# Half of the scaled copies on another engine, and lasting buffers for the decay, in a fused Mamba and convolution kernel

## The chip, the cores and the metric

The kernel runs on one core of one Trainium2 chip. The core has five engines that run their own instruction queues in order: PE (TensorE, matrix products and transposes), DVE (VectorE), ACT (ScalarE), POOL (GpSimd) and SP (SyncE, which here only issues DMAs). The metric is the device time of one execution in microseconds (us). The kernel before took 19,451.17 us, the median of three runs from 19,447.44 to 19,455.76.

In the profile PE stands for matrix products, PEld for the weight loads before them, and L12 for line 12 of the kernel.

## The reference

The input x is 4 images of 256 x 64 positions with 128 channels, all in float32. Two layers are added to it, each on a group-normalised input.

Layer 0 is a two-directional Mamba block. Each of the 64 columns of an image is a sequence of T = 256 steps. After a layer norm and a projection to 256 inner channels there comes, for each direction, a causal convolution over four taps, a SiLU, projections to a step size, and to vectors B and C of 16 states, and the selective scan:

```python
def step(h, inp):
    u_t, d_t, B_t, C_t = inp
    dA = jnp.exp(d_t[..., None] * A)
    h = dA * h + (d_t * u_t)[..., None] * B_t[:, None, :]
    y = jnp.einsum('bdn,bn->bd', h, C_t)
    return (h, y)
```

The backward direction runs the same on the reversed sequence. The two results are summed, gated and projected back; layer norms and a small MLP follow.

Layer 1 makes queries, keys and values with two products, normalises them, convolves keys and values with 3 x 7 windows into small per-position matrices, and multiplies these per position.

## The kernel before

**Tiling.** Two sequences (SG = 2) of 256 steps make a tile of 512 columns. With 256 inner channels in two halves of 128 partitions, a group G is two sequences; there are 32 groups an image and 128 in all. For each group the scan is run for 2 directions (i) and 16 states (n). One such pass is a **unit**: 128 x 32 = 4096 units, numbered k.

**What a unit does.** `rows_of_c` (L476) fetches a row of C over all partitions with a DMA from SP. `inputs` (L481) makes two operands of the scan. The first is du times B: du lies transposed, with positions on the partitions (tile duT, four blocks of 128 x 256), so that B of a block is one number a partition; ACT multiplies each block by it into the tile dbt (L487, four instructions). The second is the decay exp(A dt): ACT computes it for each half of the channels (L493, two instructions). At the start of each of the two sequences the decay must be 0, so that nothing is carried over from one to the next; since the exponential writes 255 of 256 steps, a memset on POOL (L491) sets the missing one: the first step for the forward direction, the last for the backward one. The tile "decay" comes anew from a pool of four buffers for every unit, so the memset is repeated for every unit.

`turned` (L502) transposes dbt back on PE into a PSUM bank, channels on partitions, in four 128 x 128 pieces a half (L507). Three banks, dbs, take turns. `scanned` (L510) runs the recurrence as one scan instruction a half on DVE (L519), from the decay in SBUF and dbt in PSUM; the backward direction reads and writes reversed views. `weighted` (L521) multiplies both halves by C on POOL in one instruction (L525). `added` (L527) transposes the product into the PSUM tiles y, where it accumulates over states and directions (L547).

**Order.** The main loop (from L1006) writes unit k's steps with a lead: in pass k it calls `inputs` for unit k + 3 (AHEAD = 3) after `weighted(k)`, and `added` for unit k - 2 (LAG = 2) after the transposes of unit k + 1. Between these calls it steps generators that hold all other work: `front` for the next group (norm, convolution, projections, softplus, du on POOL at L433), `back` for a finished group, `project` and `mix` for layer 1 of the images that are done. In the first image there is no layer 1 beside the scans. Where those are written decides only a first order: a scheduler in the tile framework sets the final order of each engine's queue by its own model, and puts in the semaphore waits. In the order built for the kernel before, the memset for unit k + 3 mostly stands just ahead of unit k's product on POOL.

**The end.** When all units are done, `mix_alone` (L882) works off what is left of layer 1 (136 of the 512 blocks of 128 positions). There the pool's tiles dbt and decay are reused for other data: `pair("decay")` (L935) takes two of them, which POOL fills (L938, recorded at L779).

Of the kernel before, what the change touches and what calls it, by code (L numbers as in the profile page):

```python
# [13 lines left out]
F32 = mybir.dt.float32  # L14
AF = mybir.ActivationFunctionType
ALU = mybir.AluOpType
# [16 lines left out]
COLS = 512  # L33
# [6 lines left out]
def fused_kernel(ctx: ExitStack, tc: tile.TileContext, a: dict, out: bass.AP):  # L40
    nc = tc.nc
    x = a["x"]
    B, T, N, _ = x.shape
    SG = COLS // T
# [3 lines left out]
    CB = COLS // 128  # L48
# [5 lines left out]
    AHEAD, LAG = 3, 2  # L54
# [120 lines left out]
    keep = ctx.enter_context(tc.tile_pool(name="keep", bufs=1))  # L175
# [3 lines left out]
    p4 = ctx.enter_context(tc.tile_pool(name="p4", bufs=4))  # L179
# [3 lines left out]
    dbs = [psum.tile([128, COLS], F32, name=f"db{k}") for k in range(3)]  # L183
# [3 lines left out]
    for t in hpad:  # L187
        nc.gpsimd.memset(t[:, :, 0 : KC - 1], 0.0)
        nc.gpsimd.memset(t[:, :, T + KC - 1 : PADT], 0.0)
    kv_pad = keep.tile([32, R, PADN], F32, name="kv_pad")  # L190
    nc.gpsimd.memset(kv_pad, 0.0)
    cols = [[keep.tile([128, 2, COLS], F32, name=f"cols{t}") for t in range(3)]]
# [14 lines left out]
    def take():  # L207
        return free.pop(0)

    def give(*bs):  # L210
        free.extend(bs)
# [269 lines left out]
    def inputs(G, i, n):  # L481

        st = state[G]
        dt, bT, duT = st["dt", i], st["bT"], st["duT", i]
        dbt = st["dbt", i, n] = p4.tile([128, CB, DI], F32, name="dbt")
        for j in range(CB):
            nc.scalar.mul(dbt[:, j, :], duT[:, j, :], bT[:, i, j, n : n + 1])  # L487
        da = st["da", i, n] = p4.tile([128, 2 * SG, T], F32, name="decay")
        lo = 1 - i

        nc.gpsimd.memset(da[:, :, (T - 1) * i : (T - 1) * i + 1], 0.0)  # L491
        for h in range(2):
            nc.scalar.activation(  # L493
                da[:, h * SG : (h + 1) * SG, lo : lo + T - 1],
                dt[:, h, :].rearrange("d (s t) -> d s t", s=SG)[:, :, lo : lo + T - 1],
                AF.Exp,
                scale=neg_a[i][:, h, n : n + 1],
            )
        if n == NS - 1:
            st[("half", "read")[i]] = True  # L500
# [9 lines left out]
    def scanned(k):  # L510
        G, i, n = units[k]
        st = state[G]
        hs = st["hs", i, n] = p4.tile([128, 2, COLS], F32, name="hs")
        da = st.pop(("da", i, n)).rearrange("d (h s) t -> d h (s t)", h=2)
        for h in range(2):
            d0, d1, dh = da[:, h, :], dbs[(2 * k + h) % 3], hs[:, h, :]
            if i == 1:
                d0, d1, dh = d0[:, ::-1], d1[:, ::-1], dh[:, ::-1]
            nc.vector.tensor_tensor_scan(dh, d0, d1, 0.0, ALU.mult, ALU.add)  # L519
# [209 lines left out]
    def operands(K):  # L729

        b, ci = divmod(K, NCHK)
        w = chunk[K]
        img = kv_img[b % 2]
        to = w["cols"] = cols[0]
        cols.append(cols.pop(0))
        for i in range(2):
            for t in range(3):
                c0, cn = CH0[t], CH0[t + 1] - CH0[t]
                src = img[16 * i + c0 : 16 * i + c0 + cn, :, ci * R * N : ci * R * N + COLS + 2 * N]
                tap = src.ap[1][0]  # L740
                src = bass.AP(src.tensor, src.offset, [[tap, KW * cn], [N, KH], [1, COLS]])
                nc.sync.dma_start(out=to[t][0 : TAPS * cn, i, :], in_=src)
        w["operands"] = True

    def ready(K):
        w = chunk.get(K, {})
        return w.get("projected") and (K % NCHK == NCHK - 1 or chunk.get(K + 1, {}).get("projected"))
# [28 lines left out]
    def outer(eng, pr, left, right, na, nb):  # L776

        n = pr.shape[1]
        eng.tensor_tensor(  # L779
            pr.rearrange("p e (a b) -> p e a b", b=nb),  # L780
            left[:, :, :, None].to_broadcast([128, n, na, nb]),
            right[:, :, None, :].to_broadcast([128, n, na, nb]),
            ALU.mult,
        )
# [15 lines left out]
    def by(ap, inner=16):  # L800
        return ap.rearrange("p (e a) -> p e a", a=inner)

    def loaded_x1(K):
        x1 = p1.tile([128, CB, C], F32, name="x1t")
        nc.sync.dma_start(out=x1, in_=chunk_of(im[K // NCHK]["x1d"], K % NCHK))
        return x1
# [75 lines left out]
    def mix_alone(first, project):  # L882

        blocks = [(K, j) for K in range(first, B * NCHK) for j in range(CB)]
        wk = [{} for _ in blocks]

        def pair(name):
            return [p4.tile([128, 8, 128], F32, name=name) for _ in range(2)]

        def needed(K):  # L890
            while not ready(K):
                project()
            if "operands" not in chunk[K]:
                operands(K)

        x1 = o = None
        for m in range(-1, len(blocks) + 3):
            project()
            w1 = wk[m - 1] if 0 <= m - 1 < len(blocks) else None
            w2 = wk[m - 2] if 0 <= m - 2 < len(blocks) else None  # L900
            w3 = wk[m - 3] if 0 <= m - 3 < len(blocks) else None
            if w3:
                K, j = blocks[m - 3]
                if x1 is None:
                    x1 = loaded_x1(K)
                if j == 0:
                    o = p1.tile([128, CB, C], F32, name="o")
                pr = pair("dbt")
                for h in range(2):
                    outer(nc.vector, pr[h], by(w3["vg"][:, 256:512])[:, 8 * h : 8 * h + 8], by(w3["nv"], NH)[:, 8 * h : 8 * h + 8], DV, NH)  # L910
                give(w3["vg"])
            project()
            if w1:
                bank = take()
                gathered(bank[:, 0:128], *w1["pr"])
                kt = p1.tile([128, NH * DD], F32, name="ker")
                nc.scalar.copy(kt, bank[:, 0:128])
            if w2:
                pr2 = products(w2["vg"][:, 0:256], w2["ker"], DV, NH)
                w2["nv"] = p1.tile([128, DV * NH], F32, name="nv")  # L920
                nc.vector.tensor_reduce(w2["nv"].rearrange("p (v n) -> p v n", n=NH), pr2, AX.X, ALU.add)
            project()
            if m + 1 < len(blocks):
                K, j = blocks[m + 1]
                w = wk[m + 1]
                if j == 0:
                    needed(K)
                if j == 2 and ready(K + 1) and "operands" not in chunk[K + 1]:
                    operands(K + 1)
                kb = take()  # L930
                convolved(kb[:, 0:256], 0, K, j, True)
                ks = p2.tile([128, CB, DI], F32, name="duT")[:, 0, :]
                nc.scalar.copy(ks, kb[:, 0:256])  # L933
                give(kb)
                w["pr"] = pair("decay")  # L935
                q = chunk[K]["qkv"][:, j, 0 : NH * DK].rearrange("p (n k) -> p k n", k=DK)
                for h in range(2):
                    outer(nc.gpsimd, w["pr"][h], q[:, 8 * h : 8 * h + 8], by(ks)[:, 8 * h : 8 * h + 8], NH, DD)  # L938
                if j == CB - 1:
                    chunk[K]["mixed"] = True  # L940
            project()
            if w1:
                nc.tensor.transpose(bank[:, 128:256], kt, ident)
                w1["ker"] = p1.tile([128, NH * DD], F32, name="ker2")
                nc.scalar.copy(w1["ker"], bank[:, 128:256])
                give(bank)
            if w3:
                K, j = blocks[m - 3]
                ot = take()
                gathered(ot[:, 0:128], *pr, x1[:, j : j + 1, :])  # L950
                nc.scalar.copy(o[:, j, :], ot[:, 0:128])
                give(ot)
                if j == CB - 1:
                    x1 = None
            project()
            if w1:
                K, j = blocks[m - 1]
                w1["vg"] = take()
                convolved(w1["vg"][:, 0:256], 1, K, j, True)
                convolved(w1["vg"][:, 256:512], 2, K, j, False)  # L960
            project()
            if w3 and blocks[m - 3][1] == CB - 1:
                for _ in finish(blocks[m - 3][0], o):
                    pass
# [36 lines left out]
    for k in range(AHEAD):  # L1001
        rows_of_c(*units[k])
        inputs(*units[k])
    for h in range(2):
        turned(0, h)
    for k in range(len(units) + LAG):  # L1006
# [10 lines left out]
        if k < len(units):  # L1017
            scanned(k)
            weighted(k)
# [8 lines left out]
        if k + AHEAD < len(units):  # L1028
            inputs(*units[k + AHEAD])
# [97 lines left out]
```

## Time and profile before

| | us |
|---|---|
| median of three runs | 19,451.17 |
| span of the profiled execution | 19,460.2 |
| PE busy in it | 16,890.9 (87%) |
| ACT busy | 16,112.6 (83%) |
| DVE busy | 15,851.8 (81%) |
| POOL busy | 11,465.8 (59%) |

The profiled execution's own time is its span, from the first to the last instruction; it lies within 0.05% of the median. The mean granted TensorE clock was 0.960 of full speed. A busy PE is not a PE at its peak, since matmuls are pipelined and their ends are modelled. A group's line in the profile gives, in this order, the code line, the engine and operation, the tiles written and read with their shapes, the count, the busy time in us and the mean ns of one, and last the idle time of that engine just before these instructions with what ended it. A line of the waits gives who waited, for which instruction, the us in total, how many times, and the longest.

### The profile page before, as it was taken

The page shows a single profiled execution, that of the slowest core. Times are in us where ns is not written, and L with a number is a line of the kernel's source. Part 1 is how long each engine was busy: PE and PEld are TensorE (multiplying, and loading weights), DVE is VectorE, ACT ScalarE, POOL GpSimd, SP SyncE. Part 2 cuts the span into 40 slices and gives each one's busy share as a digit, 9 for nine tenths or more (in the row PEclk, how much of TensorE's full clock was granted, in tenths as well). Part 3 has the DMA queues.
Part 4 walks back from the last instruction along what each step waited for, and adds up shares of the span by engine and source line. Part 5 has one row for each costly group of instructions (what it writes and reads, how often), then busy time and mean ns, then how long its engine had stood idle before and what let it go on. Part 6 is the DMA issues. An engine that isn't in the chain of part 4 may idle for free. (4 is left out here: it accounts for less than half of the span.)

```text
span 19460.2 us, 309441 instructions
## 1 busy us (share of the span) xinstructions
PE 16890.9 (87%) x109614; PEld 13040.6 (67%) x109614; DVE 15851.8 (81%) x13054; ACT 16112.6 (83%) x31415; POOL 11465.8 (59%) x9129
## 2 busy tenths in 40 slices
PE   6999888888888888888888888888888888888788
PEld 4666666666666666666666666666666666666677
DVE  5777777768888888888888888887888888888778
ACT  6999999998888888888888888888888888888432
POOL 4777677765556555555655555555555555565444
PEclk9999999999999999999999999999999999999899
DMA  2232223223322322322332223222232232332222
GB/s 76 86 87 86 80 81 81 80 80 87 82 80 85 85 81 80 87 81 81 87 90 84 75 80 84 77 79 78 82 83 78 78 87 78 80 87 77 73 71 65
DMA packets 1321088, 1574.83 MB, mean 81 GB/s; under 512 B 343232, under 2 KB 704880, under 8 KB 1319536
## 3 DMA queue, kind: packets, MB, share of 16 engines
q1 hardware_dynamic: 1318000, 1554.40, 28.6%
q8 instruction: 865, 14.17, 0.3%
q14 instruction: 687, 5.63, 0.1%
q10 hardware_dynamic: 1536, 0.63, 0.0%
HBM read 1420.15 MB, written 134.45 MB: 80 GB/s over the span
## 5 line engine op out<-in xcount | busy, mean ns | idle before, releaser
L525 POOL TENSOR_TENSOR hs<-hs,cc 128x1024 f32<-128x1024 f32 x4096 | 9703.4, 2372 | 6728.4 <-issue 2796.6
L519 DVE TENSOR_TENSOR_SCAN hs<-decay,db 128x512 f32<-128x512 f32 x8192 | 9513.7, 1204 | 1651.0 <-PE db L507 1125.9
L487 ACT ACTIVATE dbt<-duT,bT 128x256 f32<-128x256 f32 x16384 | 7066.9, 500 | 359.7 <-PE db L507 354.7
L493 ACT ACTIVATE decay<-dt,neg_a 128x510 f32<-128x510 f32 x8192 | 5451.5, 713 | 560.5 <-DVE hs L519 536.0
L507 PE MATMUL db<-ident,dbt 128*128 128x128 f32 x32768 | 4956.8, 282 | 958.7 <-DVE hs L519 861.8
L507 PEld LDWEIGHTS db<-ident,dbt 128*128 128x128 f32 x32768 | 3847.6, 145 | 2461.2 <-DVE hs L519 1291.2
L547 PE MATMUL y<-ident,hs 128*128 128x128 f32 x32768 | 4460.9, 279 | 25.0 <-POOL hs L525 22.8
L547 PEld LDWEIGHTS y<-ident,hs 128*128 128x128 f32 x32768 | 3853.1, 144 | 210.2 <-issue 150.4
L374 PE MATMUL mm<-hpad,w_cv 128*128 128x512 f32 x4096 | 1921.8, 597 | 70.2 <-ACT u L313 36.5
L768 DVE TENSOR_TENSOR pr<-qkv,mm 128x2048 f32<-128x2048 f32 x372 | 849.8, 2284 | 631.3 <-PE mm L763 393.4
L374 PEld LDWEIGHTS mm<-hpad,w_cv 128*128 128x128 f32 x4096 | 711.6, 190 | 678.6 <-issue 578.1
L779 DVE TENSOR_TENSOR pr<-mm,nv 128x2048 f32<-128x2048 f32 x374 | 850.7, 2275 | 131.8 <-PE mm L763 90.1
L768 DVE TENSOR_TENSOR pr<-mm,ker 128x2048 f32<-128x2048 f32 x413 | 937.7, 2270 | 15.3 <-PE mm L763 13.2
L864 DVE TENSOR_REDUCE nv<-pr 128x128 f32<-128x2048 f32 x376 | 851.9, 2266 | 1.1
L853 DVE TENSOR_REDUCE ker<-pr 128x128 f32<-128x2048 f32 x376 | 851.2, 2264 | 0.4
L790 PE MATMUL mm<-ident,pr 128*128 128x128 f32 x5968 | 754.6, 278 | 105.6 <-DVE pr L779 90.7
L790 PEld LDWEIGHTS mm<-ident,pr 128*128 128x128 f32 x5968 | 676.4, 143 | 229.2 <-DVE pr L779 103.2
L779 POOL TENSOR_TENSOR decay<-qkv,duT 128x1024 f32<-128x1024 f32 x272 | 544.9, 2030 | 406.2 <-ACT duT L933 273.2
L433 POOL TENSOR_TENSOR du<-dt,u 128x1024 f32<-128x1024 f32 x256 | 607.0, 2371 | 297.6 <-ACT dt L322 191.7
L446 PE MATMUL mm<-ident,du 128*128 128x128 f32 x2048 | 377.0, 303 | 290.4 <-POOL decay L491 149.5
L218 ACT ACT_TABLE_LOAD x419 | 537.6, 1283 | 6.8
L534 PEld LDWEIGHTS y<-diag_d,u 128*128 128x128 f32 x4096 | 495.6, 200 | 60.2 <-ACT yt L564 32.7
(288 smaller groups left out, 18950.8 us busy)
## 6 DMA issues: line engine op xcount, KB each, us to landing
cc<-cd SPq DMA_DIRECT2D x4096, 256.0 KB
cols<-kv_img SPq DMA_DIRECT2D x444, 210.0 KB
xin<-in_x SPq DMA_DIRECT2D x256, 256.0 KB
kv_img<-kv_pad SPq DMA_DIRECT2D x896, 64.0 KB
cols<-kv_img SPq DMA_DIRECT2D x222, 252.0 KB
xst<-in_x SPq DMA_DIRECT2D x128, 256.0 KB
x1d<-ot SPq DMA_DIRECT2D x256, 128.0 KB
xt<-x1d SPq DMA_DIRECT2D x128, 256.0 KB
```

What stands on the lines that cost most here:

```text
L374: nc.tensor.matmul(cv.rearrange("c (s t) -> c s t", s=SG), lhsT=w_cv[i][:, k, h * 128 : (h + 1) * 128], rhs=hp[:, :, o : o + T], start=k == 0,
L487: nc.scalar.mul(dbt[:, j, :], duT[:, j, :], bT[:, i, j, n : n + 1])
L493: nc.scalar.activation(da[:, h * SG : (h + 1) * SG, lo : lo + T - 1], dt[:, h, :].rearrange("d (s t) -> d s t", s=SG)[:, :, lo : lo + T - ...
L507: last = nc.tensor.transpose(db[:, 128 * j : 128 * (j + 1)], dbt[:, j, 128 * h : 128 * (h + 1)], ident)
L519: nc.vector.tensor_tensor_scan(dh, d0, d1, 0.0, ALU.mult, ALU.add)
L525: nc.gpsimd.tensor_tensor(hs, hs, cc[:, None, :].to_broadcast([128, 2, COLS]), ALU.mult)
L547: nc.tensor.matmul(y[j // 2][:, j % 2, h, :], lhsT=hs[:, h, 128 * j : 128 * (j + 1)], rhs=ident, is_transpose=True, start=False, stop=i == ...
L768: nc.vector.tensor_tensor(pr, left.rearrange("p (a e) -> p a e", e=16)[:, :, None, :].to_broadcast([128, na, nb, 16]), right.rearrange("p ...
L779: eng.tensor_tensor(pr.rearrange("p e (a b) -> p e a b", b=nb), left[:, :, :, None].to_broadcast([128, n, na, nb]), right[:, :, None, :].t ...
L790: nc.tensor.matmul(to, lhsT=p, rhs=ident, is_transpose=True, start=k == 0, stop=stop and k == len(blocks) - 1, skip_group_check=True,)
L853: nc.vector.tensor_reduce(ker.rearrange("p (n d) -> p n d", d=DD), pr, AX.X, ALU.add)
L864: nc.vector.tensor_reduce(nv.rearrange("p (v n) -> p v n", n=NH), pr, AX.X, ALU.add)
```

## The change

`inputs` gives two of the four copies of a unit (blocks j = 2 and 3) to POOL, as a `tensor_scalar` with the same per-partition number. The decay no longer comes from the pool: four tiles of 1028 columns are made once and set to 0 as a whole on POOL, at the start, and handed round in turn. The exponential always writes steps 1 to 255 of each sequence of 256 columns. Forward units read the tile from column 0, backward units from column 1, so a written 0 stands at the start of each sequence in the sense of the scan either way, and the memset of every unit is gone. `mix_alone` takes its "decay" pairs from the same four tiles.

```diff
+    decays = [keep.tile([128, 2 * SG * T + 4], F32, name=f"decays{k}") for k in range(AHEAD + 1)]
+    for t in decays:
+        nc.gpsimd.memset(t, 0.0)
...
         for j in range(CB):
-            nc.scalar.mul(dbt[:, j, :], duT[:, j, :], bT[:, i, j, n : n + 1])
-        da = st["da", i, n] = p4.tile([128, 2 * SG, T], F32, name="decay")
+            b_n = bT[:, i, j, n : n + 1]
+            if j < CB // 2:
+                nc.scalar.mul(dbt[:, j, :], duT[:, j, :], b_n)
+            else:
+                nc.gpsimd.tensor_scalar(dbt[:, j, :], duT[:, j, :], b_n, None, ALU.mult)
+        da = decays[0]
+        decays.append(decays.pop(0))
         lo = 1 - i
-
-        nc.gpsimd.memset(da[:, :, (T - 1) * i : (T - 1) * i + 1], 0.0)
+        st["da", i, n] = da[:, i : i + 2 * COLS]
         for h in range(2):
             nc.scalar.activation(
-                da[:, h * SG : (h + 1) * SG, lo : lo + T - 1],
+                da[:, h * COLS : (h + 1) * COLS].rearrange("d (s t) -> d s t", s=SG)[:, :, 1:T],
                 dt[:, h, :].rearrange("d (s t) -> d s t", s=SG)[:, :, lo : lo + T - 1],
                 AF.Exp,
                 scale=neg_a[i][:, h, n : n + 1],
...
-        da = st.pop(("da", i, n)).rearrange("d (h s) t -> d h (s t)", h=2)
+        da = st.pop(("da", i, n))
         for h in range(2):
-            d0, d1, dh = da[:, h, :], dbs[(2 * k + h) % 3], hs[:, h, :]
+            d0, d1, dh = da[:, h * COLS : (h + 1) * COLS], dbs[(2 * k + h) % 3], hs[:, h, :]
...
         def pair(name):
+            if name == "decay":
+                ts = [decays.pop(0) for _ in range(2)]
+                decays.extend(ts)
+                return [t[:, 0:1024].rearrange("d (e a) -> d e a", e=8) for t in ts]
             return [p4.tile([128, 8, 128], F32, name=name) for _ in range(2)]
```

## The prediction

> **What bounds the kernel now.** I read the busy time by stages first, because the whole-span shares (PE 87%, ACT 83%, DVE 81%, POOL 59%) average over stages with different limits. In the table each engine has its busy us in a stretch and, in brackets, its instructions.
>
> ```profile
> core 0: us, PE busy (x) PEld busy (x) DVE busy (x) ACT busy (x) POOL busy (x), PEclk, DMA share, GB/s
> 500.00:4800.00 4300.00, 3856.52 (x24455) 2874.37 (x24453) 3300.36 (x3240) 4118.43 (x7992) 2978.60 (x2413) 0.97 0.29 83
> 4800.00:9300.00 4500.00, 3934.73 (x25448) 3018.44 (x25448) 3816.00 (x3019) 3842.99 (x7460) 2601.69 (x2104) 0.96 0.30 83
> 9300.00:13800.00 4500.00, 3880.89 (x25063) 2992.93 (x25063) 3760.11 (x2970) 3780.81 (x7327) 2544.67 (x2062) 0.96 0.29 81
> 13800.00:18110.00 4310.00, 3755.47 (x24275) 2890.15 (x24273) 3648.68 (x2861) 3662.98 (x7116) 2485.00 (x2010) 0.96 0.29 81
> 18240.00:19460.00 1220.00, 1042.20 (x8047) 963.06 (x8045) 972.86 (x606) 368.25 (x886) 618.43 (x333) 0.92 0.25 71
> ```
>
> There are three regimes. Up to 4800 us (stage 1: the first image, no second layer beside it) ACT is 96% busy and is the bound. From 4800 to 18,110 us (stage 2) PE, ACT and DVE are all at 84 to 87%: nobody is full, and time goes in handing work over. After 18,110 us (the end piece) the changed lines don't run. One pass of the inner loop, a "unit" (one direction and one of 16 states for one pair of sequences), has one L525 product on POOL: that line counts 1148 of them in 500 to 4800 us, and 976, 957 and 931 in the three windows of stage 2. So a unit takes 4300/1148 = 3.746 us in stage 1 and 13,310/2864 = 4.647 us in stage 2.
>
> The groups give a unit's work: four dbt copies and two exponentials on ACT, two scans on DVE, one product and one memset on POOL.
>
> ```profile
> L525 POOL TENSOR_TENSOR hs<-hs,cc 128x1024 f32<-128x1024 f32 x4096 | 9703.4, 2372 | 6728.4 <-issue 2796.6 <-ACT dbt L487 862.1 <-DVE hs L519 738.1
> L487 ACT ACTIVATE dbt<-duT,bT 128x256 f32<-128x256 f32 x16384 | 7066.9, 500 | 359.7 <-PE db L507 354.7 <-DVE duT L315 1.1
> L493 ACT ACTIVATE decay<-dt,neg_a 128x510 f32<-128x510 f32 x8192 | 5451.5, 713 | 560.5 <-DVE hs L519 536.0 <-DVE bT L414 14.7 <-POOL qkv L712 7.3
> L491 POOL MEMSET decay<- 128x4 f32 x4096 | 435.8, 108 | 118.1 <-DVE hs L519 101.5 <-ACT dbt L487 16.5
> ```
>
> A dbt copy has a mean of 500 ns but neighbours overlap: 7066.9/16384 = 0.431 us of ACT each. That ACT is what PE waits for in stage 1 is seen in order of time: ACT goes from L487 to L493 to L487 without a gap, 3.02 us a unit where nothing else comes between, and the weight loads of the transposes wait for it.
>
> ```profile
> 2513.30 1.71 ACT L487 ACTIVATE dbt<-duT,bT 128x256 f32<-128x256 f32 x4
> 2513.99 0.14 PEld L507 LDWEIGHTS db<-ident,dbt 128*128 128x128 f32 x1 [0.24 <-ACT dbt L487]
> 2514.91 1.32 ACT L493 ACTIVATE decay<-dt,neg_a 128x510 f32<-128x510 f32 x2
> 2516.14 1.70 ACT L487 ACTIVATE dbt<-duT,bT 128x256 f32<-128x256 f32 x4
> 2516.68 0.14 PEld L507 LDWEIGHTS db<-ident,dbt 128*128 128x128 f32 x1 [0.28 <-ACT dbt L487]
> ```
>
> The waits of stage 2 (here 4800 to 9300 us) read otherwise: PE waits mostly for a scan to free one of three PSUM banks, DVE waits for PE, and ACT itself waits.
>
> ```profile
> DVE hs L519 <- PE db L507: 271.4, 154, 8.4
> PE db L507 <- DVE hs L519: 243.8, 251, 3.6
> ACT decay L493 <- DVE hs L519: 170.9, 162, 3.3
> ```
>
> **The change, part by part.**
>
> *ACT loses two dbt copies a unit.* 2 x 0.431 = 0.86 us. ACT work a unit goes from 4118.43/1148 = 3.59 to 2.73 us in stage 1, and from 11,286.8/2864 = 3.94 to 3.08 us in stage 2.
>
> *POOL gains two copies a unit, at a price X that the trace does not show.* No POOL instruction here multiplies one tensor by a per-partition number. From below: a memset of 256 elements, which reads nothing.
>
> ```profile
> L106 POOL MEMSET w<- 128x256 f32 x1 | 0.3, 306 | 0.0
> masks.py:199 POOL TENSOR_SCALAR_AFFINE_SELECT ident<-ident 128x128 f32<-128x128 f32 x1 | 0.3, 296 | 0.0
> L79 POOL TENSOR_SCALAR_AFFINE_SELECT group_c<-group_c 128x128 f32<-128x128 f32 x1 | 0.5, 520 | 0.0
> L589 POOL TENSOR_TENSOR xo<-xo,xg 128x512 f32<-128x512 f32 x128 | 163.7, 1279 | 40.6 <-DVE xo L586 40.6
> ```
>
> From above: the two-input product. L589 (512 elements, 1279 ns) and L525 (1024, 2372 ns) lie on 0.19 us + 2.13 ns an element, so 0.73 us for 256. Nearest is the flat one-input select of the identity, 296 ns for 128: with the same 0.19 us of start, 0.83 ns an element, so 0.40 us for 256; L79's select with a two-level pattern would give 0.85 us, but dbt and duT slices are flat. I add 0.05 us for fetching the per-partition number (an estimate, no row shows it) and take X = 0.45 us, ends 0.31 and 0.73.
>
> Here a rule speaks against the change. The Trainium skill's page "GPSIMD Engine Reference" says (section 4.1, Engine selection) not to do elementwise arithmetic there, about 2x slower than VectorE, yet that one-input operations run at about line rate; section 3.1 has 2.6 cycles an element for two inputs and 1.8 for a tight loop, at 1.2 GHz. The trace agrees on two inputs (2.13 ns is 2.56 cycles). For one input the page gives, with the trace's 0.19 us start, about 0.41 us (near one cycle) or 0.57 us (1.8 cycles), estimates. The select row sides with the first. POOL's work a unit in stage 1 is 2978.6/1148 = 2.595, less the memset's 0.107, plus 2X: 3.31, 3.39 or 3.63 us for X = 0.41, 0.45 or 0.57, against 3.746 now. By row and by line rate the change gains in stage 1; by 1.8 cycles it gains nothing there.
>
> *The memset goes.* 4096 x 0.107 us of POOL, in the sum above, and with it a wait: each scan and each exponential needed a POOL memset standing behind L525 products. Little hung on it (DVE's wait for L491 is 25.9 us in all). Four memsets of 128x1028 at the start, 4 x 0.95 us by L194's 128x1024, lie before 200 us, where POOL has 10 us of work: nothing; 4 us if uncovered. Four decay buffers rotate as before, and ACT may now write one half when the scan of that half is done. No DMA is added.
>
> *Waits that come in.* In the built order the POOL copies for unit k+4 stand mostly just ahead of the product of unit k (65% of them; 19% are for k+3, 11% for k+5). They wait until PE has transposed unit k, which that product needs anyhow, so queue order alone costs little. Behind POOL's copies stand L525 (then PE's L547) and du (L433, then PE's L446). PE's L507 needs both halves of dbt, some three to four units after POOL writes them, so POOL may lag about a unit before PE stands. PE's waits for POOL are now 124 us in stage 1 and 30 + 100 + 62 = 192 us in stage 2.
>
> **The sum.** *Stage 1:* the fullest engine after is POOL with 3.39 us a unit, PE next with 3856.5/1148 = 3.36, DVE 2.87, ACT 2.73. ACT alone at the top reached 96%; two engines as close as these I put at 94.5%: 3.39/0.945 = 3.585, gain 0.16 x 1148 = 185 us. *Stage 2:* after, PE 4.04, DVE 3.92, POOL 2.665 - 0.107 + 0.90 = 3.46 (74%), ACT 3.08 of 4.647 us. PE and DVE stay the bound; what can go is lateness of ACT: DVE's waits ended by ACT lines (75 + 95 + 113 = 283 us) and PE's (77 + 58 + 48 = 183), 466 us. ACT's slack, which works off the backlog after a run of table loads and SiLU, grows from 15% to 34%, so I take 60%: 280 us. Against it PE's 192 us of waits for POOL, growing by the load 74/57, 60 us. Net 220. *End piece and first 500 us:* nothing, or under 20 us. Sum 405 us off a span of 19,460.2; that execution lies 9 us above the median of 19,451.2, so on the median 19,046, say **19,045 us** (-2.1%).
>
> **The rivals.**
>
> *POOL becomes the bound (slower).* If X is near 0.73, stage 1 has 2.488 + 1.46 = 3.95 us on POOL; at 96% that is 4.11 us a unit, +0.37 x 1148 = +420 us; in stage 2 POOL reaches 2.558 + 1.46 = 4.02, level with PE and DVE, three engines in line again with POOL's products late for PE, say +0.05 x 2864 = +140. About 20,000 us. For: the page's "slower" rule, L79's 520 ns. Against: the flat select's 296 ns. It decides from X of about 0.6, where stage 1 gives (2.488 + 1.2)/0.945 = 3.90, +180 us, and eats what stage 2 gains.
>
> *The hand-over goes too (much faster).* If the waits between PE and DVE in stage 2 are the echo of ACT's bursts (the three scans that a late dbt holds up), PE sets the pace there at 95%: 4.04/0.95 = 4.25, -0.39 x 2864 = -1120 us, with stage 1's 230: 18,100; half of it 18,700. For: PE's weight loads wait 621 us for ACT in stage 2. Against: ACT stands idle 15% there, waiting for PE and DVE.
>
> *Nothing to see.* Stage 1 passes from ACT to POOL at the same pace (X near 0.53 does it) and stage 2 is held by three banks alone: 19,450 us.
>
> **How the numbers follow.** Forecast 54%, much faster 14%, nothing 6%, slower 26%. Faster by over 0.2% (about what a measurement of this kernel can tell from no change): 0.68; within: 0.06; slower: 0.26. The forecast's own range is 18,700 to 19,400 (X from 0.40 to 0.52, stage 2 from nothing to twice the gain). The range reaches down to 18,500, past half of the second rival, and up to 19,780, X near 0.67, leaving out about one in ten at each end.
>
> **What would show it.** POOL's new line at 0.40 to 0.52 us, 8192 of them; ACT near 75% in stage 1 and 66% in stage 2; a unit of about 3.6 us in stage 1 and 4.57 in stage 2; PE's waits for ACT's dbt mostly gone, those for POOL up. Wrong if the POOL line is over 0.6 us, if PE's L547 waits long for L525, or if stage 2 moves by several per cent though PE and DVE keep their work.

## The result, and the profile after

The changed kernel takes 20,754.3 us (median of four runs, 20,735.7 to 20,777.2) against 19,449.3 us: 1.0669 times the kernel before, 95% interval 1.0654 to 1.0684. The forecast was 19,045 us with a range up to 19,780. The profiled execution has a span of 20,734.0 us, 1274 us more than before. Almost none of that lies at the end: from the start of the last product on POOL to the end of the span it is 1348 us before (18,111.8 to 19,460.2) and 1350 us after (19,384.3 to 20,734.0).

The windows that were shown of the kernel before, with each engine's busy us and its instructions in brackets:

```profile
core 0: us, PE busy (x) PEld busy (x) DVE busy (x) ACT busy (x) POOL busy (x), PEclk, DMA share, GB/s
500.00:4800.00 4300.00, 3447.41 (x20700) 2574.96 (x20699) 2815.09 (x2807) 2834.49 (x4818) 4294.74 (x3080) 0.93 0.23 70
4800.00:9300.00 4500.00, 3809.05 (x24071) 2943.34 (x24069) 3557.25 (x2841) 3031.38 (x5268) 4108.15 (x2943) 0.94 0.26 78
9300.00:13800.00 4500.00, 3816.00 (x24502) 2929.43 (x24502) 3672.20 (x2909) 3068.45 (x5306) 4124.62 (x2956) 0.96 0.27 80
```

POOL is busy for 4294.7 of 4300 us in the first window, and 91 to 92% of the time in the other two, where it was at 57 to 58%. ACT fell to 66% and 67 to 68%.

These windows are fixed in time, but the stages are not. Layer 1 begins beside the scans at product 1103 to 1105 in every run: at 4238 us before, at 4973 us after. So the first window, which the prediction takes for the first image alone, holds some 125 units with layer 1 before and none after, and what it says of a unit is not quite like for like. The losses are therefore also counted by units, from the trace's product starts: product 1216 (counted from 0), which lies a little behind the start of layer 1 in all runs, starts at 4723.6 us before and at 5487.0 us after. Of the 1274 us, 763 are lost up to product 1216, 509 from there to the last product, and the rest at the end.

The groups name the reason:

```profile
L532 POOL TENSOR_TENSOR hs<-hs,cc 128x1024 f32<-128x1024 f32 x4096 | 9684.5, 2369 | 726.3 <-issue 210.1
L494 POOL TENSOR_SCALAR dbt<-duT,bT 128x256 f32<-128x256 f32 x8192 | 7493.6, 931 | 472.3 <-PE db L514 420.0
L492 ACT ACTIVATE dbt<-duT,bT 128x256 f32<-128x256 f32 x8192 | 3741.3, 499 | 1401.7 <-PE db L514 1203.6
L554 PE MATMUL y<-ident,hs 128*128 128x128 f32 x32768 | 4643.4, 286 | 1261.0 <-POOL hs L532 1258.2
```

A copy on POOL takes 0.931 us, twice the 0.45 us of the prediction and beyond its upper end of 0.73. The product beside it has kept its price (2369 ns, before 2372). POOL's queue in stage 1, in order of time, has no gap; a product and two copies make 4.13 us, where ACT's turn was 3.02 us before (a unit's copies and exponentials, shown in the prediction):

```profile
2517.08 2.35 POOL L532 TENSOR_TENSOR hs<-hs,cc 128x1024 f32<-128x1024 f32 x1
2519.41 1.82 POOL L494 TENSOR_SCALAR dbt<-duT,bT 128x256 f32<-128x256 f32 x2
2521.21 2.35 POOL L532 TENSOR_TENSOR hs<-hs,cc 128x1024 f32<-128x1024 f32 x1
2523.54 1.82 POOL L494 TENSOR_SCALAR dbt<-duT,bT 128x256 f32<-128x256 f32 x2
2525.34 2.35 POOL L532 TENSOR_TENSOR hs<-hs,cc 128x1024 f32<-128x1024 f32 x1
```

In the same stretch PE stands still until the products come, and so its next transposes (L514) come late:

```profile
2523.61 1.09 PE L554 MATMUL y<-ident,hs 128*128 128x128 f32 x8 [1.41 <-POOL hs L532]
2524.54 1.04 PE L514 MATMUL db<-ident,dbt 128*128 128x128 f32 x8
2527.74 1.86 PE L554 MATMUL y<-ident,hs 128*128 128x128 f32 x8 [2.16 <-POOL hs L532]
```

The scans then wait for PE. The waits from 500 to 4800 us (who waited for whom, us in total, times, longest), after:

```profile
DVE hs L526 <- PE db L514: 804.2, 540, 7.5
PE y L554 <- POOL hs L532: 479.5, 334, 4.5
ACT dbt L492 <- PE db L514: 478.4, 346, 4.9
```

The first of them was, in that window of before:

```profile
DVE hs L519 <- PE db L507: 323.1, 284, 7.8
```

By windows a unit takes 4300/996 = 4.317 us in stage 1 (before 3.746) and, over 4800 to 13,800 us, 9000/1869 = 4.815 us in stage 2 (before 9000/1933 = 4.656).

### The profile page after: what moved, and what is told of

The parts are those of the page before. It is cut to its first block, busy times and chain, and to the rows that moved or that the text cites. A ratio compares the mean times of both kernels' runs of the same rounds, so it can differ in the third digit from the quotient of the medians.

```text
span 20734.0 us, 303196 instructions
## 1 busy us (share of the span) xinstructions
PE 17191.4 (83%) x109614; PEld 13321.3 (64%) x109614; DVE 15886.4 (77%) x13054; ACT 13313.0 (64%) x23233; POOL 18591.4 (90%) x13229
## 5 line engine op out<-in xcount | busy, mean ns | idle before, releaser
L526 DVE TENSOR_TENSOR_SCAN hs<-decays,db 128x512 f32<-128x512 f32 x8192 | 9527.7, 1205 | 2576.5 <-PE db L514 2323.5
L532 POOL TENSOR_TENSOR hs<-hs,cc 128x1024 f32<-128x1024 f32 x4096 | 9684.5, 2369 | 726.3 <-issue 210.1
L494 POOL TENSOR_SCALAR dbt<-duT,bT 128x256 f32<-128x256 f32 x8192 | 7493.6, 931 | 472.3 <-PE db L514 420.0
L500 ACT ACTIVATE decays<-dt,neg_a 128x510 f32<-128x510 f32 x8192 | 5693.6, 715 | 2243.6 <-DVE hs L526 2213.1
L554 PE MATMUL y<-ident,hs 128*128 128x128 f32 x32768 | 4643.4, 286 | 1261.0 <-POOL hs L532 1258.2
L514 PE MATMUL db<-ident,dbt 128*128 128x128 f32 x32768 | 4919.9, 287 | 873.6 <-DVE hs L526 584.5
L514 PEld LDWEIGHTS db<-ident,dbt 128*128 128x128 f32 x32768 | 3982.3, 149 | 2235.0 <-DVE hs L526 1017.4
L554 PEld LDWEIGHTS y<-ident,hs 128*128 128x128 f32 x32768 | 3925.6, 148 | 1617.4 <-POOL hs L532 1491.4
L492 ACT ACTIVATE dbt<-duT,bT 128x256 f32<-128x256 f32 x8192 | 3741.3, 499 | 1401.7 <-PE db L514 1203.6
L786 POOL TENSOR_TENSOR decays<-qkv,duT 128x1024 f32<-128x1024 f32 x272 | 544.8, 2030 | 405.5 <-ACT duT L944 272.5
L316 ACT ACTIVATE duT<-mm 128x512 f32<-128x512 f32 x384 | 224.8, 592 | 501.9 <-PE mm L449 476.0
```

Source lines behind the costliest of these rows:

```text
L492: nc.scalar.mul(dbt[:, j, :], duT[:, j, :], b_n)
L494: nc.gpsimd.tensor_scalar(dbt[:, j, :], duT[:, j, :], b_n, None, ALU.mult)
L500: nc.scalar.activation(da[:, h * COLS : (h + 1) * COLS].rearrange("d (s t) -> d s t", s=SG)[:, :, 1:T], dt[:, h, :].rearrange("d (s t) -> ...
L514: last = nc.tensor.transpose(db[:, 128 * j : 128 * (j + 1)], dbt[:, j, 128 * h : 128 * (h + 1)], ident)
L532: nc.gpsimd.tensor_tensor(hs, hs, cc[:, None, :].to_broadcast([128, 2, COLS]), ALU.mult)
L554: nc.tensor.matmul(y[j // 2][:, j % 2, h, :], lhsT=hs[:, h, 128 * j : 128 * (j + 1)], rhs=ident, is_transpose=True, start=False, stop=i == ...
```

## The experiments

The theory: the loss is the price of the POOL copies. Rivals: the lasting buffers brought a wait; the copies' place in POOL's queue, or PE's wait for POOL's half of dbt, did it rather than their time; they contend with the rest of the kernel. Later runs turned to the other half of the sum, what ACT's relief is worth. The table has all but the probe, with the medians and the ratio to the kernel before, measured beside each run, with its 95% interval. "ACT" and "POOL" are the work moved in us a unit against the kernel before, from each run's own rows (the memset's 0.11 us left aside). A unit's time, "w1" from 500 to 4800 us and "w2" from 4800 to 13,800 us, is a window's length over the L525 products (by other line numbers) in it. "To 1216" and "then" are us of the profiled execution against that of before, up to the start of product 1216 and from there to the last product; these compare the same units:

```
run              us        ratio (interval)         ACT     POOL    w1      w2      to 1216   then
before           19,449                                              3.746   4.656
changed kernel   20,754    1.0669 (1.0654, 1.0684)  -0.81   +1.86   4.317   4.815   +763      +509
e1_buffers       19,339    0.9937 (0.9923, 0.9952)   0       0      3.739   4.615     -9      -119
e2_copies        20,862    1.0722 (1.0706, 1.0738)  -0.81   +1.87   4.357   4.823   +824      +560
e3_one_copy      19,302    0.9919 (0.9903, 0.9936)  -0.41   +0.93   3.720   4.622    -30      -136
e4_product       19,403    0.9973 (0.9963, 0.9984)  -0.81   +1.05   3.762   4.618    +35       -92
e5_product_one   19,000    0.9767 (0.9752, 0.9781)  -0.41   +0.62   3.641   4.559   -168      -280
e6_light_act     18,696    0.9606 (0.9590, 0.9623)  -0.58    0      3.522   4.507   -348      -420
e7_first_image   19,232    0.9885 (0.9870, 0.9900)  image 1: as e5  3.660   4.611   -130       -99
e9_spare         21,300    1.0948 (1.0932, 1.0965)   0      +1.85   4.461   4.915   +932      +892
e8_pinned        19,166    0.9850 (0.9833, 0.9866)  -0.41   +0.62   3.656   4.606   -132      -164
```

### The price of the instruction alone

```diff
+        for w in (64, 128, 256, 512, 1024):
+            pt = probe.tile([128, 1024], F32, name=f"ptr{w}")
+            for _ in range(6):
+                nc.gpsimd.tensor_scalar(pt[:, 0:w], pa[:, 0:w], ps[:, 0, :], None, ALU.mult)
...
```

> The kernel before, with 102 extra POOL instructions on scratch tiles at its start, six of each kind: one tensor times a per-partition number at 64, 128, 256, 512 and 1024 elements, the same by an immediate number and a plain copy at 128, 256 and 512, the product with a number broadcast along the row at 256, 512 and 1024, and the product of two flat tensors at 256. They price the disputed instruction alone. If its cost lies in fetching the per-partition number (a start of some 0.7 us), 512 elements take about 1.15 us and the immediate form at 256 about 0.4 us. If it lies in the elements (3.4 ns each, or 2.9 ns above a start of 0.19), 512 take 1.65 to 1.8 us, and the immediate form at 256 is as dear, about 0.9 us. If it is contention with the rest of the kernel, 256 elements take 0.4 to 0.5 us here, where nothing else runs. The time of the whole run means nothing more than the kernel before plus the probe, about 100 us.

The groups of the probe, on POOL in a stretch (23 to 109 us) where no other compute engine works ("ptr" is a tensor times a per-partition number, "imm" times an immediate, "copy" a plain copy, "bc" a product with a number broadcast along the row, "two" a product of two flat tensors):

```profile
L180 POOL TENSOR_SCALAR ptr<-pa,ps 128x512 f32<-128x512 f32 x6 | 9.4, 1562 | 0.0
L180 POOL TENSOR_SCALAR ptr<-pa,ps 128x256 f32<-128x256 f32 x6 | 5.5, 922 | 0.0
L180 POOL TENSOR_SCALAR ptr<-pa,ps 128x128 f32<-128x128 f32 x6 | 3.6, 602 | 0.0
L184 POOL TENSOR_SCALAR imm<-pa 128x256 f32<-128x256 f32 x6 | 5.1, 847 | 0.0
L195 POOL TENSOR_TENSOR two<-pa 128x256 f32<-128x256 f32 x6 | 4.3, 722 | 0.1
L192 POOL TENSOR_TENSOR bc<-pa,ps 128x256 f32<-128x256 f32 x6 | 3.7, 612 | 0.0
L192 POOL TENSOR_TENSOR bc<-pa,ps 128x512 f32<-128x512 f32 x6 | 6.2, 1038 | 0.0
L188 POOL COPY copy<-pa 128x256 f32<-128x256 f32 x6 | 2.4, 400 | 0.0
```

The copy with a per-partition number takes 0.28 us and 2.5 ns an element; the immediate form, 847 ns, is only 75 ns cheaper. So it is the elements that cost, a little less each than that guess had it (512 take 1.56 us, under the 1.65 expected), and not the fetch of the number. Contention is out: 922 ns here, 931 in the changed kernel. The surprise is the order: this one-input instruction is dearer than a product of two tensors (722 ns), and a broadcast product, which computes the same thing, takes 612.

### One part at a time

The lasting buffers alone (all four copies on ACT as before):

```diff
-            if j < CB // 2:
-                nc.scalar.mul(dbt[:, j, :], duT[:, j, :], b_n)
-            else:
-                nc.gpsimd.tensor_scalar(dbt[:, j, :], duT[:, j, :], b_n, None, ALU.mult)
+            nc.scalar.mul(dbt[:, j, :], duT[:, j, :], bT[:, i, j, n : n + 1])
```

> Lasting decay buffers alone, all four copies on ACT. Theory (the price of the POOL copies is all of the loss): the buffers are no part of it; POOL loses a memset of 0.107 us a unit where it isn't the bound, so 19,350 to 19,480 us. Rival (the buffers bring a new wait between the scan and the exponential, which the 2213 us of ACT waiting for scans in the changed kernel may show): 19,700 us or more.

19,339 us, just under the expected band: the buffers are no part of the loss, they gain 0.6%, nearly all of it behind product 1216 (119 of 128 us). The copies alone, with the decay from the pool and its memset for every unit:

```diff
-            nc.scalar.mul(dbt[:, j, :], duT[:, j, :], bT[:, i, j, n : n + 1])
+            b_n = bT[:, i, j, n : n + 1]
+            if j < CB // 2:
+                nc.scalar.mul(dbt[:, j, :], duT[:, j, :], b_n)
+            else:
+                nc.gpsimd.tensor_scalar(dbt[:, j, :], duT[:, j, :], b_n, None, ALU.mult)
```

> Half of the copies on POOL alone, the decay from the pool with its memset for every unit. Theory: POOL is the bound and now carries the memset too, 0.107 us on some 4.3 us a unit in stage 1 and less than that beyond: 20,850 to 21,150 us. Rival (the buffers have a part in the loss): under 20,500 us.

20,862 us, as the theory had it. The copies cost 7.2%, and the two parts add up: beside the same runs of the kernel before (19,459 us) 1403 us of loss less 121 us of gain is 1282, and the change lost 1305.

### The same work for POOL at other prices

One copy of four on POOL:

```diff
-            if j < CB // 2:
+            if j < CB - 1:
```

> The changed kernel with one of the four copies on POOL instead of two, so that POOL gains 0.92 us a unit, which is what the prediction's sum had put there for two. Theory (only the price was wrong): stage 1 has POOL at 2.49 + 0.92 = 3.41 us a unit, PE 3.36, ACT 3.16, so 3.6 us a unit; stage 2 has ACT at 3.51 instead of 3.94; in all 18,950 to 19,250 us. Rival (the copies' place in POOL's queue, ahead of the product, makes PE stand whatever they cost): PE's waits for POOL stay above 1000 us and the time above 19,600 us.

19,302 us: 50 us above the theory's band and far under the rival's 19,600; PE's waits for POOL, which the rival had above 1000 us, sum to 886 (2118 in the changed kernel). POOL's added 0.93 us is what the prediction had put there for two copies; ACT's relief is half of what it had. Against the buffers alone only 36 us are gained, and stage 2 gains next to nothing (17 us behind product 1216).

Two copies as one broadcast product:

```diff
-            else:
-                nc.gpsimd.tensor_scalar(dbt[:, j, :], duT[:, j, :], b_n, None, ALU.mult)
+        b_n = bT[:, i, CB // 2 :, n : n + 1].to_broadcast([128, CB // 2, DI])
+        nc.gpsimd.tensor_tensor(dbt[:, CB // 2 :, :], duT[:, CB // 2 :, :], b_n, ALU.mult)
```

> The changed kernel with its two POOL copies written as one product of 2 x 256 elements with a number broadcast along each row, which the probe prices at 1.04 us instead of 2 x 0.92. Same work on ACT and PE, same lasting buffers, POOL at 2.49 + 1.04 = 3.53 us a unit in stage 1 and 3.60 in stage 2. Theory A (the price was the only error, the rest of the prediction's sum holds): stage 1 at 3.53/0.945 = 3.74 us a unit, no gain; stage 2 gains 220; buffers 110: about 19,110 us, at most 19,250. Theory B (ACT's load does not matter in stage 2; in stage 1 POOL goes from product to copy without a gap, 2.40 + 1.0 + 0.19 of other work, at the 92.5% that the one-copy run reached: 3.85 us a unit): 19,350 to 19,550 us. Rival (queue order and waits rather than price made the loss): above 20,300 us.

19,403 us. This is the cleanest test of the price: the values, ACT's part and the buffers are those of the changed kernel, and 0.81 us a unit less on POOL takes off 1352 us. The built order is nearly the same too (63% of the copies stand just ahead of the product four units earlier, 65% in the changed kernel). The rival that queue order and waits made the loss is out. But theory A, the prediction's sum with only X mended, is out as well by 150 us: even at this price the change is worth 0.3%, less than the buffers alone. The time lies in theory B's band, but the next runs speak against B's reason, that ACT's load doesn't matter in stage 2. The POOL copies of this run:

```profile
L492 POOL TENSOR_TENSOR dbt<-duT,bT 128x512 f32<-128x512 f32 x4096 | 4268.2, 1048 | 1048.6 <-PE db L512 859.0 <-ACT decays L498 162.4 <-ACT u L316 14.4
```

One block of four as a broadcast product:

```diff
+        for j in range(CB - 1):
+            nc.scalar.mul(dbt[:, j, :], duT[:, j, :], bT[:, i, j, n : n + 1])
+        b_n = bT[:, i, CB - 1, n : n + 1].to_broadcast([128, DI])
+        nc.gpsimd.tensor_tensor(dbt[:, CB - 1, :], duT[:, CB - 1, :], b_n, ALU.mult)
```

> One block of four on POOL, as a broadcast product of 256 elements: 0.61 us a unit instead of 0.92, with lasting buffers. Stage 1: POOL 2.49 + 0.61 = 3.10 us a unit, ACT 3.16, PE 3.36, so PE leads. Theory B: stage 1 at 3.36/0.935 = 3.60 us a unit, 0.14 x 1150 = 160 us under the buffers alone, stage 2 as with the buffers alone: 19,130 to 19,280 us. Theory A (stage 2 gains by ACT's relief, half of the change's): 18,950 to 19,100 us. Rival (any copy on POOL costs as much by queueing as ACT gains): 19,300 us or more.

19,000 us, in theory A's band (from here on, "theory A" is that ACT's relief is worth something in stage 2, "theory B" that it is not); stage 2 gains, 161 us behind product 1216 against the buffers alone. It differs from e3 in nothing but the form of that one instruction on POOL (0.62 us against 0.93), with the same built order, and that is worth 302 us, in both stages. It is 2.3% faster than the kernel before and the fastest of those here that leave nothing out. Its POOL copies:

```profile
L492 POOL TENSOR_TENSOR dbt<-duT,bT 128x256 f32<-128x256 f32 x4096 | 2506.6, 618 | 1176.0 <-PE db L512 917.6 <-ACT decays L498 224.9 <-ACT u L316 16.6
```

### What ACT's relief is worth

One wide instruction on ACT in place of four, POOL untouched. All four blocks are multiplied by the number of block 0; the right numbers of the other three are left out:

```diff
-        for j in range(CB):
-            nc.scalar.mul(dbt[:, j, :], duT[:, j, :], bT[:, i, j, n : n + 1])
+        nc.scalar.mul(dbt, duT, bT[:, i, 0, n : n + 1])
```

> The lasting buffers, and the four ACT copies of a unit made one instruction of 1024 elements with the number of block 0 for all blocks; the right numbers of the other three blocks are left out. ACT loses about 0.75 us a unit (four at 0.431 against one near 1.0), nearly as much as the change took from it, and POOL gets nothing. Theory A: stage 1 at PE's 3.36 us a unit over 0.945, -0.19 x 1150, and stage 2 gains 280 us without POOL's cost: 18,850 us or less. Theory B: stage 1 gains the same 150 to 220 us, stage 2 stays within 1% of 4.58 us a unit: 19,080 to 19,220 us. Rival (POOL's part in the wait matters and ACT's not at all): stage 1 unchanged, 19,300 us.

18,696 us: theory A holds, and theory B falls. The wide instruction takes more than guessed, 1.14 us, so ACT loses 0.58 us a unit. Against the buffers alone that is worth 339 us up to product 1216 and 301 us behind it, 0.105 us a unit. The first two windows of this run, with the columns of the first table:

```profile
500.00:4800.00 4300.00, 4017.16 (x26328) 3050.75 (x26326) 3560.49 (x3462) 3763.99 (x4874) 3114.13 (x1349) 0.99 0.29 89
4800.00:9300.00 4500.00, 4027.65 (x26363) 3115.42 (x26364) 3947.10 (x3126) 3484.30 (x4700) 2642.45 (x1167) 0.97 0.29 86
```

PE is now 93% busy in the first window and 90% in the second, from 90% and 87%; ACT still has 88% and 77%. The single product on POOL for the first image only:

```diff
+            if j < CB - 1 or G >= NGRP:
+                nc.scalar.mul(dbt[:, j, :], duT[:, j, :], bT[:, i, j, n : n + 1])
```

> As the run with one broadcast product on POOL, but only for the first image; for the other three images all four copies are on ACT. Theory B (ACT's relief is worth something only in stage 1): within 60 us of that run on either side, 19,130 to 19,280 us. Theory A (it is worth something in stage 2): 60 us or more above it. Rival (POOL's copy does harm in stage 2, through PE's waits for POOL): 60 us or more below it.

19,232 us, 232 us above e5: theory A again. In stage 2 it runs much like the buffers alone (4.611 us a unit against 4.615).

### Time on POOL, or waiting for it

The changed kernel's copies once more, behind each product, into a tile that nobody reads, with all four real copies on ACT (`weights` holds the products issued so far; `issue_after` fixes the order in the queue):

```diff
+            if j >= CB // 2:
+                with tc.issue_after(weights[-1].ins) if weights else nullcontext():
+                    nc.gpsimd.tensor_scalar(spare, duT[:, j, :], bT[:, i, j, n : n + 1], None, ALU.mult)
```

> The lasting buffers with all four copies on ACT, and on POOL, behind each product, the changed kernel's two copies of 256 elements once more, into a spare tile that nobody reads. POOL carries the changed kernel's load, 2.49 + 2 x 0.92 us a unit, while ACT keeps its own and nobody waits for the copies themselves. Theory P (POOL's time alone, through products that come late, is the loss): stage 1 at 4.3 to 4.4 us a unit and stage 2 at 4.80 or more, 20,700 to 21,100 us. Rival W (in stage 2 the loss comes from PE waiting for POOL's half of dbt): stage 1 as in P, since POOL is full there, but stage 2 under 4.68 us a unit, 20,050 to 20,350 us.

21,300 us, 200 us beyond theory P's band and far from rival W's: stage 2 takes 4.915 us a unit though nobody waits for the copies. So POOL's time, by way of its late results, is enough to make the loss. Three groups of this run:

```profile
L533 POOL TENSOR_TENSOR hs<-hs,cc 128x1024 f32<-128x1024 f32 x4096 | 9682.2, 2364 | 1284.1 <-DVE hs L527 1101.6 <-PE db L515 49.5 <-issue 36.2
L495 POOL TENSOR_SCALAR spare<-duT,bT 128x256 f32<-128x256 f32 x8192 | 7566.4, 924 | 367.3
L555 PE MATMUL y<-ident,hs 128*128 128x128 f32 x32768 | 4628.7, 285 | 933.6 <-POOL hs L533 929.9
```

The 200 us have three candidates that this run does not separate. ACT kept its full load. PE waits longer for two other products on POOL, du (586 us, 236 in the changed kernel) and xo (521, 219). And POOL now stands before products for 1284 us (726 in the changed kernel), since in this fixed order it can't fill the wait for a scan with a later unit's copy. That the fixed order costs something is shown by the last run, e5 with its copy for unit k + 3 held behind the product of unit k:

```diff
+        with tc.issue_after(weights[-1].ins) if weights else nullcontext():
+            nc.gpsimd.tensor_tensor(dbt[:, CB - 1, :], duT[:, CB - 1, :], b_n, ALU.mult)
```

> The run with one broadcast product on POOL (19,000 us), with that copy held in POOL's queue behind the product of unit k when it is for unit k + 3; the scheduler had put it mostly ahead of the product of unit k for unit k + 4, where it waits for PE to transpose unit k (918 us of waits). Theory H (that wait at the head of the queue delays the products): the wait nearly goes and the time falls to 18,950 us or less. Theory I (POOL would have waited for the scan in that time anyway): the wait moves to the products, 18,960 to 19,040 us. Theory J (the copy, one unit later, makes PE wait): 19,060 us or more.

19,166 us: theory J. The copy no longer waits at all, and PE waits for it more, 365.7 us against 141.7 in e5. Two groups of this run:

```profile
L494 POOL TENSOR_TENSOR dbt<-duT,bT 128x256 f32<-128x256 f32 x4096 | 2521.5, 616 | 0.0
L514 PE MATMUL db<-ident,dbt 128*128 128x128 f32 x32768 | 4883.8, 281 | 1126.0 <-DVE hs L526 717.4 <-POOL dbt L494 365.7 <-DVE bT L418 15.0
```

The scheduler's place for the copies was the better one, and the 918 us that they waited at the head of the queue in e5 cost less than a copy that comes later: 53% of e5's copies stood just ahead of the product four units earlier, two products before their place here.

## Why the prediction was wrong

*The step that failed is X, the price of a POOL copy.* The prediction put it at 0.45 us between 0.31 and 0.73; it is 0.93. At 0.93 the sum's own line for stage 1, (2.488 + 1.86)/0.945, is a loss of 0.85 us a unit where it had a gain of 0.16. Both anchors were wrong for it. The lower guess, 0.40 us, took a one-input select for the like of a one-input multiply and added 0.05 us for the number. The upper end took the two-input product for the dearest thing that an elementwise instruction can be, and the probe has it cheaper (722 ns for 256). The one row that came near, L79's with 0.85 us, was set aside. The Trainium skill's page "GPSIMD Engine Reference", section 4.1, pointed the same way with "1-input is roughly line-rate": the plain copy agrees (400 ns for 256, 613 for 512, so 0.83 ns an element, the prediction's one cycle), the multiplication by a number, at 2.5 ns an element, does not. The rule against elementwise work on GpSimd, in the same section, would have kept from this loss; yet e5 gains against it, and no run here puts the multiplication on VectorE. What was lacking was a bound that does not rest on kinship of instructions.

*The first rival was the right one, and its measure close in part by luck.* It said that POOL becomes the bound, from X of 0.6. With 0.93, POOL's work in stage 1 is 2.488 + 1.86 = 4.35 us (the window after has 4294.7/996 = 4.31); the unit takes 4.317, and the three windows shown have POOL at 100%, 91% and 92%. Put into the rival's form, 0.93 gives 4.35/0.96 = 4.53 us a unit, 0.785 x 1148 = 900 us in stage 1, and with its 140 us in stage 2 1040 us of the 1305 measured; it had 26% and a time of 20,000. Two errors offset each other in that: counted by units, 763 us were lost up to product 1216, where the form puts 900 on stage 1 (it fills POOL to 96%, and the window has it full), and 509 us behind it, over three times the 140.

*ACT's relief was worth what the prediction said, or more.* It gave 280 us in stage 2 for ACT's lateness, for 0.86 us less ACT a unit; in e6 0.58 us less take off 301 us behind product 1216. PE, the next engine, let the first window down to 3.52 us a unit, under the 3.585 that was forecast.

*A second step failed: POOL's part in stage 2 was undersized even near the forecast price.* The prediction gave 60 us in stage 2 for PE's waits on POOL, by the load, and stage 1 the rule that the leader reaches 94.5%. e4, with 1.05 us added where the forecast had 0.90, is 64 us slower than the buffers alone; behind product 1216 it loses 27 us against them, where the forecast's sum had a net gain of 220. Between 4800 and 17,500 us PE waits for POOL 149 us with the buffers alone and 486 us in e4: 337 us more, not 60. The cost of POOL time rises with its load. From e5 to e3, 0.31 us more a unit on POOL cost 144 us behind product 1216 (16% of the added time) and 138 us up to it (36%); from e4 to the changed kernel, 0.81 us more cost 601 us (26%) and 728 us (74%).

*The buffers' gain was put at nothing* because DVE's waits for the memset sum to 26 us. They gain 121 us. Where that comes from wasn't taken apart: without the memset the exponential no longer waits for POOL, and a half may be written once its own scan is done; both went at once.

*Right were* the end piece, the built order as harmless next to the price, ACT's new load in stage 1 (2834.5/996 = 2.85 us a unit, forecast 2.73), and the sign that would show it wrong: a POOL line over 0.6 us and L547 (now L554) waiting long for L525 (now L532). In the second rival, the 230 us of stage 1 have no sum behind them; the forecast's own is 185.

## What to carry to other kernels

Before work is moved to an engine, time that very instruction there, at that size, in a dozen lines beside the kernel: the nearest rows of a trace can be of another kind, and here the whole forecast hung on one such number. A broadcast product in place of a multiply by a per-partition number made the move of one block of four a gain: with the lasting buffers it is 2.3% faster than the kernel before (the buffers alone 0.6%, the multiply in its place 0.8%). An engine at 57% of its time is no free room when others wait for its product: each us put on POOL cost a sixth to a quarter of itself behind product 1216, and up to it a third, or three quarters on the way to a full POOL. And compare stages by units of work, not by windows fixed in time: a change of speed moves the stages through the windows.

## What was not expected of the hardware

On GpSimd, per element of 128 partitions in float32: multiply by a number 2.5 ns, two-input product 2.1 ns, broadcast product 1.67 ns (612, 1038 ns for 256 and 512), plain copy 0.83 ns. The granted clock of TensorE was lower where PE was busy less: in the first window 0.97 before (PE busy 90%), 0.93 in the changed kernel (80%), 0.91 in the run with spare copies (78%), 0.99 where ACT was relieved (93%). Which of the two follows the other, and how much time it adds, was not measured apart.
